# The norms of a half of the heads, computed beside the row sums of a softmax

## The chip, the cores and the metric

The kernel runs on one core of a Trainium2 chip. The metric is the device time of one execution in microseconds (us); the number that counts is the median of several executions of the whole kernel. Everything is in fp32.

## The reference

A transformer layer over `x` of 8 batches, 512 rows and 256 features: attention with 16 heads of 64, in which queries and keys are divided by their norms, and then a gated feed-forward part. Cut to what matters here:

```
def _l2norm(t):
    return t / jnp.maximum(jnp.linalg.norm(t, axis=-1, keepdims=True), 1e-12)
xn = layernorm(x)
q, k, v = heads(xn @ w_q), heads(k of xn @ w_kv), heads(v of xn @ w_kv)
q = _l2norm(q) * jnp.exp(scale)
k = _l2norm(k)
attn = jax.nn.softmax(jnp.einsum('bhid,bhjd->bhij', q, k), axis=-1)
out = heads_joined(jnp.einsum('bhij,bhjd->bhid', attn, v))
x = x + layernorm(out @ w_out + b_out)
x = x + layernorm(ffn(layernorm(x)))
```

So each row of q and of k has one norm for each head, and each row of a softmax has one sum.

## The kernel before, in words

**Tiling and staging.** The attention part comes first, over the 8 batches, and the feed-forward part after it. The 16 heads are 8 head pairs; pairs 0 to 3 are the first half (`hf` 0), pairs 4 to 7 the second (`hf` 1). For a half of a batch there are four projections each of q and k (`qk_step`: product qp or kp in L411, a copy out of PSUM in L422, and its square into a tile called spread). `norms_step` then makes the factors of a half. TensorE multiplies the squares by a mask of halves, with the array in four 32-column tiles (pn_q or pn_k, L456). ScalarE copies the sums out (nd, L480); SyncE folds them by a DMA into a 128x32 tile (nf, L462), VectorE puts a floor under them (L488), GpSimd raises them to the power -0.5 (L312), and for q VectorE multiplies by the scale (L495). SyncE stores the result to DRAM (nq or nk, L502), loads it back spread over the partitions by two DMAs of 512 KB (spread_q or spread_k, L470), and VectorE multiplies the four blocks of qT or kT by it (L512). Scores read only the multiplied blocks.

**Units.** The attention loop runs over units, one for each batch and head pair. In a unit, TensorE gets the first two blocks of scores of the next pair (s, L541), the four blocks of values of this pair (po, L586), in every odd unit the row sums of this pair and the one before it (pd, L609, also in 32-column tiles), the last two blocks of scores of the next pair, and then whatever stands in `plan` for the unit's two slots. ScalarE takes the exponentials of the scores (L555), VectorE adds them up (es, L566). The row sums go through `inverted_two`: the copy d (L623), a fold by DMA (L651), a reciprocal (L671), a store (L657) and two DMAs that spread it (rden, L662), after which VectorE scales oT (L691).

**The plan.** Batch `b` has 16 slots from `base = b * NSLOT`. Projections of the second half stand in slots base - 2 to base + 1. Its norms stand in slot base (q, in unit 0) and base + 2 (k, in unit 1). The scores of pair 4, the first that need the second half, are issued in unit 3. The first half of the next batch is projected and gets its norms in slots base + 6 to base + 9. Slots also hold the output projection of the batch before (pa, L711, L721 to L735, and the store of its rows x1, L759), projections of v (vp, L387), layer norms of the next rows (pt_a, L344), and loads. Over the first batches the slots also hold work on the weights: loads (`looked_at`, L854), tests on VectorE (L861, L866) and `weight_sums`, sums on VectorE (L898) with stores to DRAM (L907). The tile of a sum has two buffers, so the fourth sum of a group waits for an earlier store.

**The order.** Steps are not issued directly. The class `Steps` (L34 to L136) collects them with what they read, write and take. TensorE's order is the order in which they were added; for the other engines and SyncE's queue it plans times from given lengths, and among the steps that are ready it takes the one whose due time, counted back from TensorE's steps, is the earliest. So a step of TensorE that is moved also moves what hangs on it in the orders of the four others. Each engine executes its order strictly. The buffers matter too: the copies d and nd share a pool of two, and pd, pn, pa, vp, qp, kp and pt share a PSUM pool of three.

Of the kernel before, what the change touches and what calls it, by code (L numbers as in the profile page):

```python
# [139 lines left out]
def tile_fast(  # L140
# [50 lines left out]
    NP = H // 2  # L191
# [4 lines left out]
    HP = NP // 2  # L196
# [114 lines left out]
    def power(d, n):  # L311
        nc.gpsimd.tensor_tensor(d, d, neghalf.to_broadcast([P, n]), ALU.pow)  # L312
# [132 lines left out]
    def norms_step(b, hf, which):  # L445

        n = (which, b, hf)
        pn, d, f, r = ("pn", *n), ("nd", *n), ("nf", *n), ("spread", *n)
        to = (which + "T", b, hf)
        r_dram = dram.tile([HH, S], F32, tag=f"n{which}_{b}_{hf}", name=f"n{which}_{b}_{hf}")  # L450
        NF = HH * S // P

        def products():
            tile_of(ps_w, [P, S], "w", pn)
            for j in range(HP):
                nc.tensor.matmul(  # L456
                    T[pn][ts(j, 32), :], lhsT=halves_of, rhs=T[r][:, j, :], start=True, stop=True
                )

        def folded():  # L460
            tile_of(small, [P, NF], "nf", f, bufs=2)
            nc.sync.dma_start(  # L462
                T[f],
                T[d][::16, :].rearrange("i (c n) -> i c n", c=16),
            )

        def spread():
            tile_of(spreadp, [P, HP, S], "spread", r)
            for h in range(2):
                nc.sync.dma_start(  # L470
                    T[r][ts(h, DH)],
                    r_dram.rearrange("(j h) s -> h j s", h=2)[h : h + 1].to_broadcast([DH, HP, S]),
                )

        steps.add(
            "pe", 0.86, products, reads=[(r, j) for j in range(HP)], writes=[(pn, 0)],
            takes=[("w", 3, pn)], tiling=("col", 32),
        )
        steps.add(
            "act", 0.59, lambda: nc.scalar.copy(tile_of(sqp, [P, S], "sq", d), T[pn]),  # L480
            reads=[(pn, 0)], writes=[(d, 0)], takes=[("sq", 2, d)],
        )
        steps.add(
            "sync", 0.1, folded, reads=[(d, 0)], writes=[(f, 0)], takes=[("nf", 2, f)], lag=1.8
        )
        steps.add(
            "dve", 0.12,
            lambda: nc.vector.tensor_scalar_max(T[f], T[f], NORM_FLOOR * NORM_FLOOR),  # L488
            writes=[(f, 0)],
        )  # L490
        steps.add("pool", 6.0, lambda: power(T[f], NF), writes=[(f, 0)])
        if which == "q":
            steps.add(
                "dve", 0.12,
                lambda: nc.vector.tensor_scalar(  # L495
                    T[f], T[f], escale[:, hf : hf + 1], None, ALU.mult
                ),
                reads=[("escale", 0)], writes=[(f, 0)],
            )
        steps.add(  # L500
            "sync", 0.1,
            lambda: nc.sync.dma_start(r_dram.rearrange("i (c n) -> (i c) n", c=16), T[f]),  # L502
            reads=[(f, 0)], writes=[(("rd", *n), 0)], lag=1.5,
        )
        steps.add(
            "sync", 0.2, spread, reads=[(("rd", *n), 0)], writes=[(r, j) for j in range(HP)],
            lag=7.5,
        )
        for j in range(HP):
            steps.add(  # L510
                "dve", 0.69,
                lambda j=j: nc.vector.tensor_tensor(  # L512
                    T[to][:, j, :], T[to][:, j, :], T[r][:, j, :], ALU.mult
                ),
                reads=[(r, j)], writes=[(to, j)],
            )

    def v_step(b, hf, t):
        pm, to = ("vp", b, hf, t), ("v", b, hf)
        projected(pm, b, t, wkv_sb, INNER + hf * HALF)  # L520

        def copied():
            if t == 0:
                tile_of(vp, [P, NT, HALF], "v", to)
            nc.scalar.copy(T[to][:, t, :], T[pm])

        steps.add(
            "act", 0.59, copied, reads=[(pm, 0)], writes=[(to, t)],
            takes=[("v", 2, to)] if t == 0 else (),
        )  # L530
# [109 lines left out]
    def inverted_two(b, p):  # L640

        d = row_sums(b, (p, p + 1), P // 4)
        f, r = ("fold", b, p), ("rden", b, p)
        r_dram = dram.tile([4, S], F32, tag=f"r_{b}_{p}", name=f"r_{b}_{p}")
        T["r", b, p], T["r", b, p + 1] = (r, 0), (r, 1)

        def folded():
            tile_of(small, [P, S // 32], "fold", f, bufs=1)  # L650
            nc.sync.dma_start(  # L651
                T[f],
                T[d][::32, :].rearrange("k (c n) -> k c n", c=32),
            )

        def stored():
            nc.sync.dma_start(r_dram.rearrange("k (c n) -> (k c) n", c=32), T[f])  # L657

        def spread():
            tile_of(esp, [P, 2, S], "rden", r, bufs=1)  # L660
            for h in range(2):
                nc.sync.dma_start(  # L662
                    T[r][ts(h, DH)],
                    r_dram.rearrange("(i h) s -> h i s", h=2)[h : h + 1].to_broadcast([DH, 2, S]),
                )

        steps.add(
            "sync", 0.3, folded, reads=[(d, 0), (d, 1)], writes=[(f, 0)],
            takes=[("fold", 1, f)], lag=1.8,
        )  # L670
        steps.add("dve", 0.2, lambda: nc.vector.reciprocal(T[f], T[f]), writes=[(f, 0)])  # L671
        steps.add("sync", 0.1, stored, reads=[(f, 0)], writes=[(("rd", b, p), 0)], lag=1.5)
        steps.add(
            "sync", 0.3, spread, reads=[(("rd", b, p), 0)],
            writes=[(r, c) for c in range(2)], takes=[("rden", 1, r)], lag=4.0,
        )
# [89 lines left out]
    plan = {}  # L766

    def at(slot, step):
        plan.setdefault(slot, []).append(step)

    def qk_plan(b, hf, slots, norm_slots, between=None):


        for w, some, n in zip("qk", (slots[:HP], slots[HP:]), norm_slots):
            for j, s in enumerate(some):
                at(s, lambda w=w, j=j: qk_step(b, hf, w, j))
            if w == "k" and between:
                at(n, between)
            at(n, lambda w=w: norms_step(b, hf, w))

    def v_plan(b, hf, slots):
        for t, s in enumerate(slots):
# [7 lines left out]
    for b in range(B):  # L790
        base = b * NSLOT
        next_rows(b + 1, base, (0, 2))
        if b:
            qk_plan(b, 1, [base + s for s in (-2, -2, -1, -1, 0, 0, 1, 1)], (base, base + 2))
        next_rows(b + 1, base, (1, 3))
        if b:
            v_plan(b, 1, [base + s for s in (3, 5, 6, 7)])
            for t in range(NT):
                at(base + 2 + t, lambda b=b, t=t: out_proj(b - 1, t))
            n = b - 1 + NX  # L800
            if n < B:
                at(base + 6, lambda n=n: loads(n))
            elif n < B + 2:
                at(base + 6, lambda c=n - B: reloads(c))
        if b + 1 < B:
            qk_plan(
                b + 1, 0, [base + s for s in (6, 6, 7, 7, 8, 8, 9, 9)], (base + 8, base + 9),
                lambda b=b: v_step(b + 1, 0, 0),
            )
            for t in range(1, NT):  # L810
                at(base + 10 + t, lambda b=b, t=t: v_step(b + 1, 0, t))

# [154 lines left out]
    for k, u in enumerate(units):  # L967
        ahead = units[k + 1 : k + 2]
        for jb in range(1, NT):
            summed(*u, jb)  # L970
        for g in range(2):
            for n in ahead:
                for jb in (2 * g, 2 * g + 1):
                    scores(*n, jb)
            if g == 0:
                for jb in range(NT):
                    values(*u, jb)
                if not ahead:
                    for t in range(2):
                        out_proj(B - 1, t, (0, NP - 1), tail=True)  # L980
                b, p = u
                if (b, p // 2) == (B - 1, HP - 1):
                    inverted(b, p)
                elif p % 2:
                    inverted_two(b, p - 1)
        for g in range(2):
            for step in plan.pop(2 * k + g, []):
                step()
        values_out(*u)
        if (b, p // 2) == (B - 1, HP - 1):  # L990
            normalised(b, p)
        elif p % 2:
            normalised(b, p - 1)
            normalised(b, p)
    assert not plan
    for t in range(2, NT):
        out_proj(B - 1, t, (0, NP - 1), tail=True)
    for t in range(NT):
# [1010 lines left out]
```

## Time and profile before

| | |
|---|---|
| median of three runs | 1638.92 us (1638.04 to 1640.67) |
| the profiled execution | 1637.79 us |
| its span | 1636.0 us |
| mean granted TensorE clock | 0.994 |
| busy: TensorE, VectorE, ScalarE, GpSimd | 98%, 62%, 54%, 30% |
| waits of TensorE for keys (L541 for L512) | 10.9 us, 2 times |
| period of a batch, from 305.12 us on | 125.44 us |

Times inside the execution count from the start of the span. A line of the timeline gives the start, the length, engine, line, operation, what is written and read, and the number of instructions taken together; in brackets stands the idle time before it and what ended it. An fp32 product leaves two records, so four products of pn are eight records.

### The profile page before, as it was taken

To read this page: it belongs to the slowest core of one execution; us is meant where nothing else is said; L and a number is where in the kernel's file an instruction comes from. 1 tells how busy PE (TensorE), PEld (TensorE's weight loads), DVE (VectorE), ACT (ScalarE), POOL (GpSimd) and SP (SyncE) were. 2 spreads that over 40 slices of the span, in tenths; PEclk is the share of its full clock that TensorE was granted. 3 is DMA by queue.
4 is the path that set the end of the run, shared out by engine and by line. 5 is a ranking of instruction groups with operands and counts; after the bars stand their busy time and mean duration, and the time that the engine had idled before them with its cause. 6 is when DMAs were issued, how large, how long until landed. Compare 5 with 4: busy or idle time off the path is not lost.

```text
span 1636.0 us, 18863 instructions
## 1 busy us (share of the span) xinstructions
PE 1606.2 (98%) x6808; PEld 916.7 (56%) x6808; DVE 1022.2 (62%) x1708; ACT 878.1 (54%) x1343; POOL 487.6 (30%) x356
## 2 busy tenths in 40 slices
PE   9998989999999999999999999999999999999997
PEld 4332443343353353353353353788888888888886
DVE  3586687454363363364353465869786987879686
ACT  4664535535635535635635534466566646664663
POOL 4211123122122122113112120357155416534451
PEclk9999999999999999999999999999999999999999
DMA  6445455222132122132131231433524532452440
GB/s 176 118 143 154 146 178 147 54 78 67 41 74 65 42 71 67 34 86 57 37 92 47 48 84 35 142 109 136 155 65 130 166 116 78 132 164 65 129 154 28
DMA packets 91042, 159.91 MB, mean 98 GB/s; under 512 B 23868, under 2 KB 39484, under 8 KB 86844
## 3 DMA queue, kind: packets, MB, share of 16 engines
q1 hardware_dynamic: 71324, 95.71, 22.0%
q0 software_dynamic: 18912, 61.87, 12.3%
q8 instruction: 55, 0.90, 0.2%
q10 hardware_dynamic: 704, 1.05, 0.2%
q14 instruction: 47, 0.39, 0.1%
HBM read 140.26 MB, written 17.56 MB: 96 GB/s over the span
## 4 chain that ended last, share of the span: by engine, by line
PE 83%; DVE 2%; issue 1%; DMA 1%; ACT 1%; POOL 0%; SPq 0%; DVEq 0%
PE g L1262 25%; PE s L541 12%; PE po L586 12%; PE p L1188 6%; PE pa L711 6%; PE vp L387 5%; PE kp L411 5%; PE qp L411 5%; PE py L1376 3%; PE pd L609 2%; PE pn_q L456 1%; PE pn_k L456 1%; DMA spread_k<-nk 0%; POOL nf_k L312 0%; PE ptf L1132 0%
## 5 line engine op out<-in xcount | busy, mean ns | idle before, releaser
L555 ACT ACTIVATE e<-s 128x1024 f32<-128x1024 f32 x256 | 248.4, 1021 | 129.6 <-PE s L541 128.7
L541 PE MATMUL s<-qT,kT 64*128 64x512 f32 x1024 | 258.3, 623 | 12.5 <-DVE kT L512 10.9
L586 PE MATMUL po<-e,v 128*64 128x512 f32 x1024 | 235.3, 602 | 0.0
L1262 PE MATMUL g<-h,wb_S 128*128 128x512 f32 x1024 | 234.3, 389 | 0.0
L312 POOL TENSOR_TENSOR nf_q<-nf_q,neghalf 128x32 f32<-128x32 f32 x16 | 87.9, 5494 | 453.6 <-DVE nf_q L488 438.4
L1262 PEld LDWEIGHTS g<-h,wb_S 128*128 128x128 f32 x1024 | 192.0, 188 | 39.8
L566 DVE TENSOR_TENSOR es<-es,e 128x1024 f32<-128x1024 f32 x128 | 156.6, 1224 | 90.0 <-ACT e L555 85.2
L541 PEld LDWEIGHTS s<-qT,kT 64*128 64x128 f32 x1024 | 88.8, 188 | 167.0 <-issue 124.6
L1262 PE MATMUL g<-h,wb_A 128*128 128x512 f32 x768 | 176.4, 389 | 0.0
L1262 PEld LDWEIGHTS g<-h,wb_A 128*128 128x128 f32 x768 | 143.9, 188 | 29.8
L586 PEld LDWEIGHTS po<-e,v 128*64 128x64 f32 x1024 | 68.1, 137 | 160.9 <-issue 158.8
L566 DVE TENSOR_TENSOR es<-e,e 128x1024 f32<-128x1024 f32 x64 | 78.3, 1223 | 116.8 <-PE pd L609 96.3
L1080 DVE TENSOR_TENSOR h<-C,h 128x512 fp32r<-128x512 f32 x112 | 129.6, 1213 | 3.9 <-ACT h L1070 3.8
L1080 DVE TENSOR_TENSOR h<-B,h 128x512 fp32r<-128x512 f32 x112 | 107.9, 1004 | 27.0 <-ACT h L1070 26.7
L312 POOL TENSOR_TENSOR nf_k<-nf_k,neghalf 128x32 f32<-128x32 f32 x16 | 89.3, 5580 | 118.7 <-issue 97.8
L387 PE MATMUL vp<-wkv_sb,aT 128*128 128x512 f32 x256 | 120.6, 602 | 0.0
L711 PE MATMUL pa<-wo_sb,oT 128*128 128x256 f32 x512 | 117.2, 382 | 0.0
L411 PE MATMUL kp<-aT,wkv_sb 128*128 128x512 f32 x256 | 115.8, 601 | 1.4 <-ACT kT L422 1.4
L1318 POOL TENSOR_TENSOR B<-B,B 128x512 f32<-128x512 f32 x64 | 101.9, 1621 | 43.7 <-DVE B L1219 38.8
L411 PE MATMUL qp<-aT,wq_sb 128*128 128x512 f32 (+1 forms) x272 | 114.3, 570 | 0.0
L681 ACT COPY oT<-po 128x512 f32<-128x512 f32 x64 | 37.5, 586 | 141.5 <-PE po L586 141.5
L711 PEld LDWEIGHTS pa<-wo_sb,oT 128*128 128x128 f32 x512 | 95.9, 190 | 31.1 <-issue 17.8
(133 smaller groups left out, 2078.8 us busy)
## 6 DMA issues: line engine op xcount, KB each, us to landing
wb_S<-s POOLq DMA_DIRECT2D x32, 1024.0 KB, 5.2
spread_q<-nq SPq DMA_DIRECT2D x32, 512.0 KB
spread_k<-nk SPq DMA_DIRECT2D x32, 512.0 KB
rden<-r SPq DMA_DIRECT2D x62, 256.0 KB
wb_A<-in_h1T_dram POOLq DMA_DIRECT2D x12, 1024.0 KB, 5.6
wb_A<-in_h2T_dram POOLq DMA_DIRECT2D x12, 1024.0 KB, 5.6
s<-sum SPq DMA_DIRECT2D x32, 256.0 KB
w<-in_h1T_dram SPq DMA_DIRECT2D x8, 512.0 KB
```

Of the source, the lines that this page charges most:

```text
L312: nc.gpsimd.tensor_tensor(d, d, neghalf.to_broadcast([P, n]), ALU.pow)
L387: nc.tensor.matmul(pm, lhsT=T["aT", b][:, c, ts(t, P)], rhs=w[:, c, c0 : c0 + HALF], start=(c == 0), stop=(c == ND - 1),)
L411: nc.tensor.matmul(T[pm][:, cols], lhsT=w[:, c, c0 : c0 + P], rhs=T["aT", b][:, c, cols], start=(c == 0), stop=(c == ND - 1),)
L541: nc.tensor.matmul(T[s][:, h, :], lhsT=T[kT][hp, j, ts(jb, P)], rhs=T[qT][hp, j, :], start=True, stop=True,)
L555: lambda: nc.scalar.activation(tile_of(ep, [P, 2, S], "e", e), T[s], AF.Exp),
L566: nc.vector.tensor_tensor(T[t], T["e", b, p, 0] if jb == 1 else T[t], T["e", b, p, jb], ALU.add)
L586: nc.tensor.matmul(T[po][h * DH : (h + 1) * DH, :], lhsT=T[v][:, jb, c0 : c0 + DH], rhs=T[e][:, h, :], start=(jb == 0), stop=(jb == NT - 1),)
L711: nc.tensor.matmul(banks(), lhsT=T["oT", b, p][:, ts(t, P)], rhs=wo_sb[:, p, :], start=(p == 0), stop=(p == NP - 1),)
L1080: lambda: nc.vector.tensor_tensor(T[h][:, 1, c, :], T[raw][:, c, :], T[h][:, 0, c, :], ALU.subtract),
L1188: nc.tensor.matmul(T[ps[k]], lhsT=(w1r, w2r)[k][c][:, ts(o, P)], rhs=row_halves(b, i)[0][:, c, :], start=(c == 0 and i == 0), stop=(c == N ...
L1262: nc.tensor.matmul(T[to[o]], lhsT=T[w][:, c, ts(o, P)], rhs=T[h][:, i, c, :], start=(first and c == 0 and i == 0), stop=(c == NQ - 1 and i ...
L1318: lambda: (nc.gpsimd if T_ENGINE == "pool" else nc.vector).tensor_tensor(T[dst][:, c, :], T[x][:, c, :], T[y][:, c, :], ALU.subtract),
```

## The change

For the second half of each batch from batch 1 on, the norms of q and of k no longer stand in slots base and base + 2. Both are added directly behind the row sums of pairs 0 and 1, in unit 1 of the batch, so TensorE executes pd, pn_q, pn_k and then the last two blocks of scores. The three groups use the same 32-column tiling. The norms of q come one unit later than before, those of k before two blocks of scores rather than after them. Each step of `norms_step` moves with them. The norms of first halves stay in their slots, and batch 0 is not touched.

```
+    beside = {}
+
+    def qk_plan(b, hf, slots, norm_units, norm_slots):
-        for w, some, n in zip("qk", (slots[:HP], slots[HP:]), norm_slots):
+        for i, (w, some) in enumerate(zip("qk", (slots[:HP], slots[HP:]))):
             for j, s in enumerate(some):
                 at(s, lambda w=w, j=j: qk_step(b, hf, w, j))
-            if w == "k" and between:
-                at(n, between)
-            at(n, lambda w=w: norms_step(b, hf, w))
+            norms = lambda w=w: norms_step(b, hf, w)
+            if norm_units:
+                beside.setdefault(norm_units[i], []).append(norms)
+                continue
+            if w == "k":
+                at(norm_slots[i], lambda: v_step(b, hf, 0))
+            at(norm_slots[i], norms)
...
         if b:
-            qk_plan(b, 1, [base + s for s in (-2, -2, -1, -1, 0, 0, 1, 1)], (base, base + 2))
+            qk_plan(b, 1, [base + s for s in (-2, -2, -1, -1, 0, 0, 1, 1)], (b * NP + 1, b * NP + 1), ())
...
-            qk_plan(
-                b + 1, 0, [base + s for s in (6, 6, 7, 7, 8, 8, 9, 9)], (base + 8, base + 9),
-                lambda b=b: v_step(b + 1, 0, 0),
-            )
+            qk_plan(b + 1, 0, [base + s for s in (6, 6, 7, 7, 8, 8, 9, 9)], (), (base + 8, base + 9))
...
                 elif p % 2:
                     inverted_two(b, p - 1)
+                for step in beside.pop(k, ()):
+                    step()
...
-    assert not plan
+    assert not plan and not beside
```

## The prediction

> **What bounds the kernel now.** I read the page's busy shares and the chain first, to see which engine sets the end.
>
> ```profile
> PE 1606.2 (98%) x6808; PEld 916.7 (56%) x6808; DVE 1022.2 (62%) x1708; ACT 878.1 (54%) x1343; POOL 487.6 (30%) x356
> PE 83%; DVE 2%; issue 1%; DMA 1%; ACT 1%; POOL 0%; SPq 0%; DVEq 0%
> ```
>
> TensorE works 98% of the span, and nearly all of the chain runs through it. So the change can save only what PE itself loses between instructions, and it can cost only where something PE needs comes late. The waits of PE name the one thing that ever came late:
>
> ```profile
> PE s L541 <- DVE kT L512: 10.9, 2, 6.8
> ```
>
> Two scores waited for the scaled keys kT: stall A (6.82 us, before 147.11) and stall B, in batch 1, with this in the timeline of PE and in the table by stretches (after the stretch: length, then busy us of PE, PEld, DVE, ACT, POOL; granted clock, DMA share, GB/s):
>
> ```profile
> 220.36 3.78 PE L541 MATMUL s<-qT,kT 64*128 64x512 f32 x8 [4.13 <-DVE kT L512]
> 216.00:220.00 4.00, 0.23 (x2) 0.00 (x0) 1.52 (x3) 0.00 (x0) 0.00 (x0) 0.97 1.06 307
> 221.00:223.00 2.00, 2.00 (x6) 0.73 (x4) 1.93 (x6) 0.53 (x1) 0.00 (x0) 0.50 0.44 177
> 226.00:227.00 1.00, 1.00 (x6) 0.21 (x4) 0.97 (x3) 0.00 (x0) 0.34 (x1) 0.72 0.03 10
> ```
>
> Eight records of s take 3.78 here and 1.99 elsewhere, because the clock is at half from about 219.9 to 226.4. The second half's pn_q of batches 1 and 2 start at 172.47 and 305.12, 132.65 apart; later ones are 125.44 apart. So stall B costs 7.2: 4.13 of idling and 3.07 of slow clock. Last, the timeline of PE in a steady batch (5), where the change sits:
>
> ```profile
> 681.45 1.07 PE L456 MATMUL pn_q<-spread_q,halves_of 128*32 128x512 f32 x8
> 682.44 3.70 PE L411 MATMUL kp<-aT,wkv_sb 128*128 128x512 f32 x8
> 690.67 1.99 PE L541 MATMUL s<-qT,kT 64*128 64x512 f32 x8
> ...
> 696.17 1.06 PE L609 MATMUL pd<-es,ones 128*32 128x512 f32 x8
> 699.08 1.07 PE L456 MATMUL pn_k<-spread_k,halves_of 128*32 128x512 f32 x8
> 725.14 1.99 PE L541 MATMUL s<-qT,kT 64*128 64x512 f32 x8
> ```
>
> After the change pn_q and pn_k follow pd at once. The s at 725.14 is the first that reads the new qT and kT: it is the deadline. Today pn_q starts 43.7 before it; then it starts 28 before.
>
> **What it saves on PE.** A group in the 32-column tiling (pn or pd, 8 records) starts its successor 0.99 to 1.00 later, each time after a change of tiling. Where no tiling changes, a record streams in 0.428 (vp at 719.88, 4 records, next start 1.71 later); the eight of pn, four side by side, would take 2 x 0.428 = 0.86. So pn_q and pn_k behind pd save 0.14 each. The kp behind pn_q takes 3.54 to its successor, qp behind vp 3.43 (735.38 to 738.81): 0.11 more. Per batch 0.39; bounds 0.11 (a stream behind pd still pays its own start) and 0.45. Seven batches (1 to 7; batch 0's second half lies elsewhere): -2.7, bounds -0.8 and -3.2.
>
> **What a steady batch then has to reach.** u counts from pd's start. The steps after it, each by its row in batch 5 or the next like it: d's copy ends u 1.74 (697.33 and 0.58), the copy of q's norms 2.57; SP issues fold(d), then q's fold 2.60; its floor on VectorE 2.06 behind, 4.66; GpSimd's power 5.42 long, 4.92 to 10.34, k's power right behind it to 16. The two rden loads, now ahead of nq on SP, go out at u 6.1 and land 5.05 later (738.81 to 743.78 gave 4.97; the mean of seven is 5.26), and on VectorE oT times rden stands ahead of q's escale: escale not at 10.4 but at 11.15 + 0.61; so nq is issued at 12.04, spread_q 1.46 later at 13.5. From here batch 0 has the pattern, one spread behind the other (first SP's issues, then VectorE):
>
> ```profile
> 32.75 1.33 SPq L470 DMA_DIRECT2D spread_q<-nq  x2
> 38.47 0.33 SPq L502 DMA_DIRECT2D nk<-nf_k  x1
> 40.47 1.23 SPq L470 DMA_DIRECT2D spread_k<-nk  x2
> ...
> 48.30 2.50 DVE L512 TENSOR_TENSOR kT<-kT,spread_k 128x512 f32<-128x512 f32 x4 [5.48 <-DMA spread_k<-nk]
> ```
>
> Issue to issue 7.72, so spread_k at u 21.2; 7.83 to kT, u 29.05; 0.84 from the first kT to PE (219.52 to 220.36): u 29.9. The deadline is 725.14 - 696.17 = 28.97, plus two pn groups of 0.86 moved in, less the pn_k of 1.00 moved from behind pd's scores: 29.68. (It drifts little: kp and pt of unit 0 lie before pd.) Late by 0.2, or 0.4 with the mean rden of 5.26; I take 0.4, bounds -0.6 (in time) and +1.2, from the spread of the rden rows (4.82 to 5.96) and as much again for the two spreads. Before, the same wait had 725.14 - 719.31 - 0.84 = 5.0 in hand. Six batches (2 to 7): +2.4, from 0 to +7. The late keys hold up only these scores; the clock stays whole at such gaps.
>
> **Here the skill's rule decides.** Today nk at 709.14 is followed by spread_k at 711.54, 2.4 later, with little else in the queue. By that row alone nk, ready at u 16, would free spread_k at 18.4, the scores at 27: no wait, and the sum of the steady batches would be the saving only. "DMA: Bandwidth & Descriptors", Queues, rings and completion order, says that each DMA engine consumes descriptors in the order of the ring; a small store behind a megabyte of spread then waits for all of it. This trace sides with it: the store of a sum issued right behind spread_q released VectorE only 7.0 later.
>
> ```profile
> 187.51 1.25 SPq L470 DMA_DIRECT2D spread_q<-nq  x2
> 188.86 0.55 SPq L907 DMA_DIRECT2D s<-sum  x1
> ...
> 195.83 0.69 DVE L898 TENSOR_TENSOR sum<-w,sum 128x512 f32<-128x512 f32 x1 [8.63 <-DMA s<-sum]
> ```
>
> So I keep 21.2. While nk queues, SP itself stands at the wait before spread_k, and behind it four x1 stores, the load of the next rows and, in batch 1, the weight stores.
>
> **Batch 1.** There weight sums (L898) share VectorE and SP. In the changed order, VectorE's sum_1_2_4 stands ahead of the first qT, and it needs the buffer of sum_1_2_3, whose store stands on SP behind spread_k, an x1 store, a weight load and another x1 store. With pd at 186.06 and the steps above (nq 198.1): spread_q 199.95, spread_k 207.75, the store 210.2. Stores behind a spread released VectorE 8.3 after the spread's issue (187.51 to 195.83) and 8.5 (124.40 to 132.89): with 0.7 for the extra load, about 217. Then sum 0.61, qT 0.61, two additions 2.27, a small one 0.34, three qT 1.85 and 0.84: PE restarts at 223.6. It runs dry at 215.74 (216.23 less the savings): 7.9 idle instead of 4.13. After it the slow clock: "TensorE: Matmul & The Clock Gate", Part 1, gives one window of about 3.4 at half speed, which is 1.7 lost; the rows show 3.07 behind stall B and about 2.2 behind stall A. I take 2.6: 10.5 against 7.2, +3.3 (by the rule +2.4). Bounds: -6.6 (no stall left) and +6. Stall A lies ahead of the change.
>
> **At nothing or nearly.** Batch 2's first half: nk's fold is now issued ahead of nq, spread_q about 1.4 later, against slack of some 0.3 where rows stand around 281: +0.3. POOL's power for the output rows now waits behind k's (5.5): VectorE's L732, ahead of the first qT, then waits to u 16.6, but qT has no data before 21; the exponentials behind k's norm copy on ScalarE wait about 1 us for fold(d), covered by the scores in flight; pd, pn_q and pn_k hold all three buffers of their PSUM pool, but the next takers come at about u 4.6, 8.2 and 9.9, and the copies free them at 1.74, 2.57 and 5.4. Without that cover each would cost about 1 us per batch.
>
> **Sum.** -2.7 + 2.4 + 3.3 + 0.3 = +3.3. The profiled execution took 1637.79 (span 1636.0), 1.1 under the median 1638.92. On the scale of the median: 1642.2, which is the forecast.
>
> **Rivals.** (1) A gain. The decision lies in one wait, sum_1_2_4: if its store lands before spread_k is issued (x1 stores and sums earlier than I reckon), batch 1 keeps kT in time like the steady ones, and the 7.2 of stall B go. Then -2.7 - 6.6 and steady batches on time: about 1630, faster. For it: later batches have slack near zero, not minus 4. Against it: SP is in order, and spread_k stands ahead of the store. 0.17. (2) A draw. The steady batches just make it (spreads 0.5 faster), B grows by 1 to 3: -2.7 + 2 + 0.3, about 1638.5 to 1641; within 0.2%. For it: the miss of 0.4 is within its own error. 0.33. (3) My forecast and its worse end: from 1642.2 on. If each steady batch misses by 1.2, 6 x 1.2 + 3.3 - 2.7 gives +8, 1647. Late from u 29.7 on, each 0.1 costs 0.6. 0.50. That the change does not bring the groups together can't be: the order on PE is fixed, pd, pn_q, pn_k, s.
>
> **How the numbers follow.** 0.2% is 3.3 us, about what a measurement of this kernel can tell from no change. Faster is under 1635.6: rival 1, 0.17. Same 0.33, slower 0.50. The range leaves out rival 1's lower part and the worst tenth: 1634 to 1649. The slower case's own range is 1642 to 1648.
>
> **What would show it.** pd, pn_q and pn_k one behind another with starts about 0.86 apart, and kp without its 0.11; "PE s L541 <- DVE kT L512" with about eight entries, most under 1 us; in batch 1 a stall of 7 to 9 us around 216 to 224 with VectorE held at L898's line by a store, and the clock at half behind it. I am wrong if steady batches never wait (then -2.7 shows whole), if spread_k is issued within 3 of nk's readiness, or if batch 1's stall is under 4.

## The result

The changed kernel takes 1643.76 us (median of 8 runs, 1642.7 to 1645.85) against 1638.85 for the kernel before (8 runs in the same comparison). The ratio is 1.0031, with a 95% interval of 1.0021 to 1.0040: slower by 4.9 us, where 3.3 was forecast. The span of the profiled execution went from 1636.0 to 1641.9.

The page of the changed kernel, busy shares and chain:

```profile
PE 1603.2 (98%) x6808; PEld 918.9 (56%) x6808; DVE 1021.0 (62%) x1708; ACT 878.2 (53%) x1343; POOL 485.9 (30%) x356
PE 42%; issue 30%; POOL 9%; DMA 6%; DVE 5%; ACT 1%; SPq 0%; POOLq 0%; DVEq 0%
```

TensorE's busy time fell by 3.0 us while the span grew by 5.9. The chain now leaves TensorE and runs through GpSimd's powers and the DMAs in the steady batches (2 to 7, in which the work on the weights is over): work off TensorE sets the time there. The waits of TensorE name it:

```profile
PE s L541 <- DVE kT L512: 20.5, 8, 10.2
```

Eight waits instead of two. One is the old stall A before batch 1 (6.62); one is batch 1's stall, now 10.24; six are new, one in each of batches 2 to 7 (0.45, 0.58, 0.71, 0.88, 0.26 and 0.79; called the steady waits below). The timeline of TensorE in batch 5:

```profile
699.70 1.06 PE L609 MATMUL pd<-es,ones 128*32 128x512 f32 x8
700.58 1.04 PE L456 MATMUL pn_q<-spread_q,halves_of 128*32 128x512 f32 x8
701.44 1.04 PE L456 MATMUL pn_k<-spread_k,halves_of 128*32 128x512 f32 x8
702.41 1.99 PE L541 MATMUL s<-qT,kT 64*128 64x512 f32 x8
...
730.34 1.99 PE L541 MATMUL s<-qT,kT 64*128 64x512 f32 x8 [0.88 <-DVE kT L512]
```

The three groups, and the scores behind them, follow one another at 0.88, 0.86 and 0.97: 2.71 together, where the kernel before paid about 2.99 (0.99 to 1.00 for each). The gain that the change is built on is there. It is smaller than the wait in the last line.

Batch 1 in TensorE's timeline and in the stretches (length, busy us of PE, PEld, DVE, ACT and POOL, granted clock, DMA share, GB/s):

```profile
225.56 3.79 PE L541 MATMUL s<-qT,kT 64*128 64x512 f32 x8 [10.24 <-DVE kT L512]
```

```profile
218.00:220.00 2.00, 0.00 (x0) 0.00 (x0) 1.09 (x2) 0.00 (x0) 0.00 (x0) 0.82 0.02 6
224.00:226.00 2.00, 0.45 (x2) 0.48 (x4) 2.00 (x5) 0.00 (x0) 0.00 (x0) 0.50 0.00 0
228.00:230.00 2.00, 2.00 (x8) 0.43 (x6) 1.87 (x7) 1.32 (x2) 1.44 (x2) 0.62 0.00 0
```

The clock falls to half within the stall, at 219.3 by the mean of its stretch (0.82 over 2 us leaves 0.72 at half), and is whole again at 229.5.

**Where the 5.9 us are.** From pd of unit 3 in batch 5 to pd of unit 1 in batch 6 the time fell from 90.97 to 89.78 (pn_q and its switch have left); from pd of unit 1 to pd of unit 3 in batch 5 it rose from 34.47 to 36.14, 0.88 of it the wait. Without the wait that is -1.19 + 0.79 = -0.40 a batch, -2.8 in seven. The six steady waits are +3.67. Batch 1's stall is 6.11 longer (10.24 against 4.13), and the slow clock behind it costs 1.91 instead of 3.01 (the scores and values after it take 7.41 to the next pd, against 8.51 before and 5.50 at full clock): +5.0. The sum is +5.9. Taken from landmark to landmark there are small shifts besides, 0.45 less up to batch 1 and about 0.5 more behind it, which cancel.

### The profile page after: what moved, and what is told of

It reads as the page before. It is cut to its first block, busy times and chain, and to the rows that moved or that the text cites. A ratio compares the mean times of both kernels' runs of the same rounds, so it can differ in the third digit from the quotient of the medians.

```text
span 1641.9 us, 18867 instructions
## 1 busy us (share of the span) xinstructions
PE 1603.2 (98%) x6808; PEld 918.9 (56%) x6808; DVE 1021.0 (62%) x1708; ACT 878.2 (53%) x1343; POOL 485.9 (30%) x356
## 4 chain that ended last, share of the span: by engine, by line
PE 42%; issue 30%; POOL 9%; DMA 6%; DVE 5%; ACT 1%; SPq 0%; POOLq 0%; DVEq 0%
PE g L1267 25%; PE p L1193 6%; POOL nf_k L312 4%; POOL nf_q L312 4%; PE py L1381 3%; DMA spread_k<-nk 3%; PE po L586 3%; DMA nk<-nf_k 2%; PE s L541 2%; DVE es L566 1%; PE pa L711 1%; PE pd L609 1%; PE vp L387 1%; DMA s<-sum 0%; PE kp L411 0%
## 5 line engine op out<-in xcount | busy, mean ns | idle before, releaser
L1323 POOL TENSOR_TENSOR C<-C,C 128x512 f32<-128x512 f32 x64 | 94.1, 1495 | 27.7 <-DVE h L1085 27.2
```

What stands on the lines that cost most here:

```text
L1323: lambda: (nc.gpsimd if T_ENGINE == "pool" else nc.vector).tensor_tensor(T[dst][:, c, :], T[x][:, c, :], T[y][:, c, :], ALU.subtract),
```

## The experiments

Each kernel was compared with the kernel before on the same chip; times are medians, ratios are against the kernel before with their 95% intervals. A profile shows one execution, which can lie off the median.

**One half of the change at a time.** `k_only` keeps q's norms in unit 0, `q_only` keeps k's norms behind the scores of unit 1:

```
-qk_plan(b, 1, [...], (b * NP + 1, b * NP + 1), ())
+qk_plan(b, 1, [...], (None, b * NP + 1), (base, None))        # k_only
+qk_plan(b, 1, [...], (b * NP + 1, None), (None, base + 2))    # q_only
```

> Only k's norms of the second half stand behind the row sums; q's stay in unit 0 as before. My theory (the tiling saves 0.4 us a batch; q's late chain, with k's spread queued behind q's, costs more): the order is pd, pn_k, s, so one change of tiling less, 0.14 to 0.2 us in each of seven batches, about 1 us; k's factors start 3 us earlier than before, so no steady batch waits for kT; batch 1 keeps a stall of about 4 us as before, since SyncE's fold of k's norms still stands behind a store of a weight sum that comes late. Total 1637 to 1639, the kernel before less 1. Rival (any group put behind the row sums jams ScalarE's two copy buffers and the PSUM pool, whichever it is): steady batches wait for kT by some tenths here too, 1640 to 1643.

> Only q's norms of the second half stand behind the row sums; k's stay behind the last two score blocks of unit 1 as before. My theory: q's factors start 14 us later than before and k's spread stays queued behind q's, so the misses of the changed kernel stay whole: 0.3 to 0.9 us in each of the six steady batches and a stall near 10 us in batch 1, where VectorE's fourth sum still stands ahead of qT; saved on TensorE is about 0.3 a batch instead of 0.4. Total 1643 to 1645.5, as the changed kernel or 1 above it. Rival (the two groups together are what is late, because GpSimd's two powers run back to back): with k's norms 3 us later the misses change by more than 1 us a batch either way, 1638 or 1650.

`k_only`: 1642.84 us, ratio 1.0018 (1.0009 to 1.0027). `q_only`: 1644.66, ratio 1.0028 (1.0017 to 1.0039). The waits of TensorE of `k_only`, with its last stall in the timeline, and then the waits of `q_only`:

```profile
PE s L541 <- DVE kT L512: 17.2, 3, 7.6
```

```profile
286.99 3.79 PE L541 MATMUL s<-qT,kT 64*128 64x512 f32 x8 [5.22 <-DVE kT L512]
```

```profile
PE s L541 <- DVE kT L512: 19.8, 8, 6.9
```

(In both, a guard for `None`, not shown, leaves the norms of that half in their slot.)

In which steady batches wait, both came out as expected. `k_only` has no wait from its batch 2's second half on; `q_only` has six, of 0.37 to 2.31, three of them above the 0.9 expected, and its stall in batch 1, 6.25, is shorter than the 10 expected (the profiled execution took 1646.49, the longest of its seven). It is q's move that makes the steady batches late. Both rivals fell: k's group behind the row sums jams nothing, and with k's norms, and so GpSimd's second power, 3 us later the waits stay.

The total of `k_only` was missed by 4 us. Its profiled execution (1645.17, above the median; the 14 lie between 1639.5 and 1647.2) shows something that neither theory had: a third stall of 5.22, ahead of batch 2's first scores. On its VectorE a weight sum waits for a store (ends at 247.89 + 0.69, against 243.49 + 0.69 in the kernel before); the floor of q's norms stands behind it and a row of tests on the weights, at 259.47 instead of 255.06, while pn_q stands at the same place (249.55 and 249.70). A move of the norms also shuffles the weight work in the fixed orders, and here that cost as much as the move itself. So the weight sums had to be taken out of the question.

**The fourth weight sum in place.** It reads the second sum and therefore takes the third sum's buffer, whose store it waits for. Written over the half of the weight tile that it reads, it needs no buffer:

```
-            s = ("sum", n, k, j)
+            s = ("sum", n, k, j) if j < 4 else w2
...
-                nc.vector.tensor_tensor(tile_of(sump, [P, HALF], "s", s), part(x), part(y), op)
+                o = part(x) if j == 4 else tile_of(sump, [P, HALF], "s", s)
+                nc.vector.tensor_tensor(o, part(x), part(y), op)
...
-            ... nc.sync.dma_start(sums_dram[n, j][:, k, :], T[s])
+            ... nc.sync.dma_start(sums_dram[n, j][:, k, :], T[s][:, :HALF])
-                takes=[("s_", 2, s)],
+                takes=[("s_", 2, s)] if j < 4 else (),
```

> The changed kernel, with the fourth weight sum of a group written over the first half of its second weight tile, so that it no longer takes the buffer of the third sum and waits for its store. My theory: in batch 1 VectorE no longer stands before qT until that store has landed behind k's spread; kT is ready when its spread lands, near 217, and the stall of 10.2 falls to 2 to 3.5 with the clock whole, so about 8 to 9 us are gained there; the stall of 6.6 before batch 1 (at 140 to 147), where the fourth sum stands in the same way behind q's spread, falls to 3 or so, 3 to 6 us gained. Steady batches keep their misses of 0.3 to 0.9. Total 1629 to 1633. Rival (in batch 1 it is the spreads themselves that are late, not VectorE): the stall stays over 7 and the total over 1637.

> The kernel before with the same edit of the fourth weight sum. My theory: its stall of 4.1 in batch 1 comes from the same wait one unit earlier (VectorE held 8.6 us until a sum's store lands behind q's spread, and k's fold on SyncE behind it), so it goes entirely, 7.2 us with the slow clock; the stall before batch 1 shrinks as in the changed kernel. Total 1626 to 1629, under the changed kernel with the same edit by 2 to 5: steady misses of 3.7 and what is left of batch 1's stall, less 3 saved on tilings. Rival (stall B of the kernel before is the spread of k itself, late by its place in the plan): it stays near 4, total 1632 to 1635.

The changed kernel so: 1632.33, ratio 0.9945 (0.9932 to 0.9958). The kernel before so: 1620.97, ratio 0.9892 (0.9878 to 0.9906). The waits of the first, and its stall in batch 1:

```profile
PE s L541 <- DVE kT L512: 10.3, 7, 3.6
```

```profile
209.77 3.67 PE L541 MATMUL s<-qT,kT 64*128 64x512 f32 x8 [3.12 <-DVE kT L512]
```

Batch 1's stall fell from 10.24 to 3.12, as expected, but the clock was not whole behind it: the eight records took 3.67, not 1.99. Stall A went entirely, where half was expected; a stall of 3.58 stands before batch 2's first scores, and five steady waits of 0.50 to 0.89 remain. The kernel before has no wait for kT left at all, and is 18 us faster with this edit, 5 below the expected range. Both its stalls went with VectorE's waits for the store of a sum (23.3 us in seven, none left). The rival, late spreads by themselves, fell for the kernel before, and holds for what remains in the changed one (3.12: spread_k goes out at 200.68 and its kT starts at 208.93, with VectorE idle 4.43 for it).

**Only k, sums in place.**

> Only k's norms behind the row sums, and the fourth weight sum in place. My theory: with the weight sums out of the way, k_only's extra stalls (7.6, 4.4 and 5.2 us before batch 1, in it and before batch 2's first scores) go, as they did for the kernel before with the sums in place (1620.97); one change of tiling less in seven batches leaves 1 us: 1619.5 to 1621. Rival (k's group behind the row sums is late by itself, through the copy that waits for the fold of the row sums): a wait for kT in the steady batches, 1623 or more.

1626.43, ratio 0.9930 (0.9908 to 0.9951), but its six runs lie between 1620.9 and 1632.7. The profiled one (span 1620.4) has one wait for kT, of 1.14, ahead of batch 2's first scores, and none in a steady batch. The wide spread was not expected.

**Only k, from batch 2 on, sums in place,** leaves the orders of the weight phase alone:

```
-qk_plan(b, 1, [...], (b * NP + 1, b * NP + 1), ())
+qk_plan(b, 1, [...], (None, b * NP + 1) if b > 1 else (), (base, base + 2))
```

> The fourth weight sum in place, and only k's norms behind the row sums, from batch 2 on; batch 1 as before. My theory: one tiling change less in six batches and no wait for kT from batch 3 on: 0.13 to 0.15 each, 0.8 to 0.9 us under the kernel before with the sums in place, 1620 to 1621; the spread of k_in_place (1620.9 to 1632.7) came from batch 1 and the weight work there, and goes. Rival (the spread comes from k's early norms in every batch): waits for kT in steady batches, or runs over 1626.

1621.54 (1620.43 to 1622.1), ratio 0.9900 (0.9884 to 0.9915). No wait for kT. The period of a batch is 125.30 (from pn_q of a second half, 288.51, to the next, 413.81), against 125.44 with the sums in place alone: 0.14 for the one switch. The median is 0.5 above the expected range and not told apart from that of the sums in place alone: the saving shows in the period only. The spread has gone in these four executions, which points to batch 1 and the weight work; which transfer there varies from run to run stays open.

**The change from batch 2 on,** once with the weight sums as they were and once in place:

```
-qk_plan(b, 1, [...], (b * NP + 1, b * NP + 1), ())
+qk_plan(b, 1, [...], (b * NP + 1, b * NP + 1) if b > 1 else (), (base, base + 2))
```

> The changed kernel with batch 1's norms put back into their old slots, the weight sums untouched: the change in batches 2 to 7 only. My theory: batch 1's stall falls from 10.2 to about 4 with 3 of slow clock behind it, 5 us less than the changed kernel, less 0.4 of tiling that is lost again; the steady waits stay (3.5 to 4 in six batches). Against the kernel before: 6 x 0.42 saved, 3.7 waited, so 0.5 to 2 us slower, 1639 to 1641. Rival (batch 1 is only the first of the late spreads, with the same cause as the others): 1643 to 1644, no gain over the changed kernel.

> The fourth sum in place, and both norms behind the row sums in batches 2 to 7 only; batch 1 as in the kernel before. This is the change without the weight work. My theory: 6 x 0.42 us of tiling and start saved, six waits for kT of 0.3 to 0.9 (sum 3 to 4.5): net +0.5 to +2 against the kernel before with the sums in place, 1621.5 to 1623; waits for kT in six places and nowhere else. Rival (the changed kernel lost only through batch 1): 1618.5, no waits.

`batch_1_as_before`: 1639.6, ratio 1.0004 (0.9995 to 1.0014), within its expectation; the stall of batch 1 is back to 3.91, and four steady waits remain. So what batch 1 adds is about 4 of the 4.9 us, and the steady batches alone come out about even. `both_from_batch_2`: 1623.7, ratio 0.9905 (0.9891 to 0.9919), 2.7 above the kernel before with the sums in place and 0.7 above its expected range. Its profile, of the slowest of the four executions (1626.4), has five waits for kT, only three of them in steady batches (0.84, 0.57 and 1.10); the other two (0.59 and 0.94) stand in batch 1 and ahead of batch 2. "Nowhere else" was wrong.

**Which link makes the steady batches late.** Two kernels take one link each out of `both_from_batch_2`. In the first GpSimd issues nk on its own queue; in the second GpSimd scales q's factors right behind its power, so that VectorE's multiplication no longer stands behind the wait for rden:

```
+        apart = which == "k" and hf and b
         steps.add(
-            "sync", 0.1,
-            lambda: nc.sync.dma_start(r_dram.rearrange(...), T[f]),
+            "pool" if apart else "sync", 1.0 if apart else 0.1,
+            lambda: (nc.gpsimd if apart else nc.sync).dma_start(r_dram.rearrange(...), T[f]),
...
+        def powered():
+            power(T[f], NF)
+            if which == "q":
+                nc.gpsimd.tensor_tensor(T[f], T[f], escale[:, hf : hf + 1].to_broadcast([P, NF]), ALU.mult)
```

> As both_from_batch_2, with one thing more: the store nk of k's factors (16 KB) is issued by GpSimd on its own queue, right behind the power, instead of by SyncE behind spread_q. My theory (nk waits in SyncE's ring until spread_q's megabyte is through, then SyncE needs its 0.5 to 1 us to issue spread_k): nk lands while spread_q runs, spread_k is issued about 3 us after nk, at 18 to 19.5 after the row sums instead of 21.5, its data follows spread_q's without a gap, and the waits for kT vanish: 1618 to 1619.5. Rival (the 16 engines are simply full: the small store waits as long on another queue): spread_k is issued at 21 or later, the waits stay, 1621.5 to 1623.

> As both_from_batch_2, with one thing more: the multiplication of q's factors by the scale is done by GpSimd right behind the power, instead of by VectorE behind the product of oT with rden. My theory (q's factors lie about 1.5 us between the end of the power and VectorE's multiplication, which stands behind a wait for rden): nq goes out 0.5 to 1 us earlier, everything behind it too, and the six waits for kT shrink from 0.3 to 0.9 to 0 to 0.3: 1618.5 to 1620.5. Rival (rden's half megabyte of data holds nq back in the ring, not VectorE): spread_q is issued at the same time after the row sums, 13.8, and the waits stay, 1621.5 to 1623.

`from_2_nk_by_gpsimd`: 1622.78, ratio 0.9905 (0.9891 to 0.9919), as without it. Batch 5 in its timeline of GpSimd and of SyncE, and nk's row in its list of transfers (the last figure is us from issue to landing):

```profile
694.85 0.60 POOL L503 DMA_DIRECT2D nk<-nf_k  x1 [0.29 <-POOL nf_k L312]
```

```profile
692.84 1.25 SPq L470 DMA_DIRECT2D spread_q<-nq  x2
700.70 1.23 SPq L470 DMA_DIRECT2D spread_k<-nk  x2
```

```profile
nk<-nf_k POOLq DMA_DIRECT2D x1, 16.0 KB, 5.8
```

The 16 KB take 5.8 us on a queue of their own, and spread_k still goes out 7.9 behind spread_q: my theory of the ring fell as the explanation. What both cases share is spread_q's megabyte on the DMA engines. The same kernel shows GpSimd's queue without it: in batch 1, where q's norms keep their old slot, spread_q had left 16 us before nk. Here are nk in GpSimd's timeline and in the list of transfers, and then the stretches in which the DMA engines run dry, in batch 1 and in batch 5 (length, PE busy, clock, DMA share, GB/s):

```profile
192.82 0.74 POOL L503 DMA_DIRECT2D nk<-nf_k  x1 [0.31 <-POOL nf_k L312]
nk<-nf_k POOLq DMA_DIRECT2D x1, 16.0 KB, 2.8
```

```profile
194.50:195.00 0.50, 0.50 (x4) 1.00 0.37 125
699.00:699.50 0.50, 0.50 (x6) 1.00 0.46 78
```

In batch 1 it took 2.8, beside the rest of rden's data; in batches 2 to 7 it took 5.1 to 6.3, on the same queue. In each of the seven it landed about 1 us after the engines had run dry. So it is not the queue that is slow: the small store waits while other data fills the engines, whichever queue it is on.

`from_2_scale_by_gpsimd`: 1627.76, ratio 0.9936 (0.9923 to 0.9948). Batch 5 in its timelines of GpSimd and SyncE (pd starts at 685.50), and the stall that it gained:

```profile
695.86 0.24 POOL L494 TENSOR_TENSOR nf_q<-nf_q,escale 128x32 f32<-128x32 f32 x1
```

```profile
696.12 0.32 SPq L504 DMA_DIRECT2D nq<-nf_q  x1
```

```profile
272.09 3.68 PE L543 MATMUL s<-qT,kT 64*128 64x512 f32 x8 [4.01 <-DVE kT L514]
```

nq goes out at 10.62 behind pd, and of the six steady waits one is left, of 0.31; the period is 124.97. This theory held for the steady batches. The total is worse all the same: 1.74 before batch 1 and 4.01 before batch 2 are new. Here every q factor was scaled on GpSimd, first halves and batch 1 too; this run alone does not show that this is the reason, but the last kernel below bears it out.

**The same link alone, in the changed kernel and in the best version.** The scale moves to GpSimd only for second halves from batch 2 on:

```
+        apart = which == "q" and hf and b > 1
...
+            if apart:
+                nc.gpsimd.tensor_tensor(T[f], T[f], escale[:, hf : hf + 1].to_broadcast([P, NF]), ALU.mult)
```

> The changed kernel with one thing more: from batch 2 on, the second half's q factors are scaled by GpSimd right behind the power, not by VectorE behind the wait for rden. Elsewhere nothing is moved, unlike from_2_scale_by_gpsimd, where every q factor was scaled so and the first scores of batch 2 came late. My theory: nq goes out at 10.6 after the row sums instead of 12.3, and the six steady waits of 0.3 to 0.9 vanish; batch 1's stall of 10 stays. Changed kernel less 3.7: 1639 to 1641. Rival (other batches' waits only move to the next late thing): 1642 or more, with waits for qT or for e.

> All that was learnt: the fourth weight sum in place, both norms behind the row sums from batch 2 on, and there the scale by GpSimd right behind the power. My theory: the savings on tilings stay alone in the steady batches, a period near 124.97 instead of 125.44, as from_2_scale_by_gpsimd's profile had it, and nothing is lost around the weights: the kernel before with the sums in place (1620.97) less 6 x 0.45, 1617.5 to 1619.5. Rival (what from_2_scale_by_gpsimd lost in batch 2's first scores comes with the scale's place in the steady batches): 1622 or more.

`changed_scale_by_gpsimd`: 1641.9, ratio 1.0021 (1.0014 to 1.0028). Its waits, and batch 1's stall:

```profile
PE s L553 <- DVE kT L524: 17.6, 5, 9.6
```

```profile
227.11 3.78 PE L553 MATMUL s<-qT,kT 64*128 64x512 f32 x8 [9.57 <-DVE kT L524]
```

Two steady waits remain (0.41 and 0.36) of six: 0.77 against 3.67. The median is 1.9 under the changed kernel's, not 3.7, and so 0.9 above the expected range; a new wait of 0.53 ahead of batch 2 is part of that, and so is stall A, 6.68 long, in the profiled execution, behind which the clock was at half for longer than in the changed kernel (the granted clock of the 20 us from 140 is 0.74 against 0.83).

`best_from_2`, with the sums in place and both norms behind the row sums from batch 2 on: 1619.5 (1618.11 to 1620.46), ratio 0.9885 (0.9868 to 0.9901), the fastest kernel of the study. Its page's busy shares, batch 5 in the timelines of SyncE and TensorE (pd at 677.18), and pn_q of batches 2 and 3:

```profile
PE 1599.8 (99%) x6808; PEld 917.7 (57%) x6808; DVE 1021.1 (63%) x1702; ACT 878.2 (54%) x1343; POOL 486.5 (30%) x362
```

```profile
687.73 0.32 SPq L514 DMA_DIRECT2D nq<-nf_q  x1
689.20 1.24 SPq L470 DMA_DIRECT2D spread_q<-nq  x2
693.10 0.33 SPq L514 DMA_DIRECT2D nk<-nf_k  x1
696.91 1.23 SPq L470 DMA_DIRECT2D spread_k<-nk  x2
```

```profile
706.87 1.99 PE L553 MATMUL s<-qT,kT 64*128 64x512 f32 x8
```

```profile
303.14 1.04 PE L456 MATMUL pn_q<-spread_q,halves_of 128*32 128x512 f32 x8
428.12 1.04 PE L456 MATMUL pn_q<-spread_q,halves_of 128*32 128x512 f32 x8
```

TensorE is busy 99% of the span, nq goes out at 10.55 and spread_k at 19.73 behind pd, the scores find their keys without a wait, and the period is 124.98 (303.14 to 428.12): the 0.46 a batch that the change can give. The new waits of `from_2_scale_by_gpsimd` are gone too, with the scale moved from batch 2 on only. Nearly all of the 19 us against the kernel before comes from the sums in place; against that edit alone the intervals of the ratios overlap, and the change's own share is shown by the period, not by the medians. The two profiles say why: the attention part's last pd starts 2.66 earlier than with the sums in place alone, but the span is only 1.3 shorter. The last pd, the end of two short gaps behind it and a stretch (columns as for the changed kernel) in this kernel, then the last pd with the sums in place alone:

```profile
1002.42 1.08 PE L621 MATMUL pd<-es,ones 128*64 128x512 f32 x4
1023.93 0.50 PE L1204 MATMUL p<-fT,wr 128*128 128x512 f32 x1 [0.99 <-DVE B L1235]
1025.69 0.50 PE L1204 MATMUL p<-fT,wr 128*128 128x512 f32 x1 [0.56 <-ACT sg L1225]
1026.00:1030.00 4.00, 4.00 (x12) 3.12 (x11) 3.56 (x6) 3.18 (x7) 0.00 (x0) 0.57 1.08 345
```

```profile
1005.08 1.08 PE L609 MATMUL pd<-es,ones 128*64 128x512 f32 x4
```

In this execution the clock fell to half for 3.4 us in the feed-forward part, which the change does not touch (0.57 over the 4 us from 1026). It followed the two gaps, of 0.99 and 0.56. The kernel with the sums in place alone has the same two gaps and kept its whole clock there.

## Why the prediction was right, point by point

Every term had the right sign. The saving was sized well, the two costs were too small, and of the links named in the steady chain one, the order within SyncE's ring, does not decide, since another queue was no faster. That the kernel got slower did not hang on the close call of the steady batches, since batch 1 alone outweighs the saving (+5.0 against -2.8); that the loss came out above the 3.3 us which the prediction takes for no change did, since without the steady waits some 2 us would have been left. Within batch 1 two errors partly cancelled: the idling was 2.3 longer than forecast, the slow clock behind it cost 0.7 less.

**The saving** was sized at 0.39 a batch and measured at 0.40, and at 0.46 where nothing is late: the row of the streaming rate (0.428 a record) priced it well. That it could not pay in the changed kernel was the deciding judgement, and it held.

**The steady chain.** Counted from pd in batch 5, forecast and measured: escale on VectorE 11.76 and 12.08, nq 12.04 and 12.34, spread_q 13.5 and 13.80, nk 16 and 15.61, spread_k 21.2 and 21.51, kT 29.05 and 29.80; the deadline of the scores, which start 0.84 behind kT, 29.68 and 29.76. The lines of SyncE and VectorE:

```profile
705.90 1.78 SPq L662 DMA_DIRECT2D rden<-r  x2
712.04 0.32 SPq L502 DMA_DIRECT2D nq<-nf_q  x1
713.50 1.24 SPq L470 DMA_DIRECT2D spread_q<-nq  x2
715.31 0.33 SPq L502 DMA_DIRECT2D nk<-nf_k  x1
721.21 1.23 SPq L470 DMA_DIRECT2D spread_k<-nk  x2
```

```profile
711.17 0.69 DVE L691 TENSOR_TENSOR oT<-oT,rden 128x512 f32<-128x512 f32 x1 [1.79 <-DMA rden<-r]
711.78 0.23 DVE L495 TENSOR_SCALAR nf_q<-nf_q,escale 128x32 f32<-128x32 f32 x1
729.50 2.50 DVE L512 TENSOR_TENSOR kT<-kT,spread_k 128x512 f32<-128x512 f32 x4 [2.40 <-DMA spread_k<-nk]
```

The whole chain came 0.3 late by the wait for rden, and spread_k took 8.29 to the first kT in batch 5, not 7.83. Six waits of 0.61 on average stand where 0.4 was taken: +3.67 for +2.4. The experiments confirm the link that was named, escale behind rden, and weaken the other: nk does wait for spread_q, but a queue of its own didn't free it, so the order within one ring, on which the prediction leaned, is not needed to explain the wait.

**Batch 1** was the term that was sized worst: +3.3 forecast, +5.0 measured. The stall came out at 10.24 for 7.9, the slow clock behind it at 1.91 for 2.6. The mechanism was as described (the row of s<-sum takes two stores together; the first, at 211.63, is the one that the sum waits for):

```profile
218.91 0.69 DVE L901 TENSOR_TENSOR sum<-w,sum 128x512 f32<-128x512 f32 x1 [12.52 <-DMA s<-sum]
```

```profile
208.65 1.24 SPq L470 DMA_DIRECT2D spread_k<-nk  x2
...
211.63 8.32 SPq L910 DMA_DIRECT2D s<-sum  x2
```

The store landed at 218.9, not 217. spread_q went out at 199.67 and spread_k 8.98 behind it, where 7.72 had been taken from a batch without weight traffic. A sum's store of 256 KB had gone out 0.4 ahead of spread_q; at the 219 and 253 GB/s of the stretches from 200 and from 204 us that is an estimated 1.0 to 1.2 us of data. In `sums_in_place_after`, with two such stores beside it, the pair took 9.77 (190.91 to 200.68).

**The slow clock** was weighed between 1.7 (an estimate from the window in the Trainium skill, "TensorE: Matmul & The Clock Gate", Part 1) and the 2.2 to 3.07 of two stalls; 2.6 was taken, and 1.91 measured. Here that estimate was nearer. The half clock ends 4.0 after the restart here and 6.2 after it in the kernel before (0.72 in the last stretch shown there puts its end at 226.56), so one stall's price is not that of the next.

**The small ones.** The first half of batch 2 cost 0.07 instead of 0.3. No new wait of TensorE for PSUM, for ScalarE's copies or for what hangs on GpSimd's row powers appeared. Rival 1, a gain by sum_1_2_4 coming in time, did not occur by itself; `sums_in_place_after` made it so, and 7.1 of the 10.2 us of that stall went, not all: spread_k itself is then what is late.

## What to carry to other kernels

Before work is regrouped to save a switch, count forward from its new place to the first reader: a chain of small transfers with hops between engines can be as long as the slack, and then a saving of 0.4 buys a wait of 0.6. Look in such a chain for an instruction that stands behind a wait for something else in an in-order engine; moving that one instruction to the engine that has the data made the same regrouping pay its 0.46 a batch. And look at background work in the same queues: the sums that waited for a store cost 18 us, more than every part of this change, and moves of other work shifted where they hurt.

## What the runs showed of the hardware

A 16 KB store took 5.1 to 6.3 us on GpSimd's queue while a megabyte of spread was in flight from SyncE's, and 2.8 on the same queue beside less data; with its queue nearly empty SyncE's own nk was followed by its reader 2.4 later. The slow clock came in steps: by the means of the stretches it lasted from 219.28 to 229.52 in the changed kernel (10.24), from 219.76 to 226.56 in the kernel before (6.80), and there in stall A from 144.64 to 151.46 (6.82). These are three and two times 3.41, which is the window that the Trainium skill gives ("TensorE: Matmul & The Clock Gate", Part 1: free-running, 3413 ns). How much of it falls behind the restart is then a matter of phase: 1.91 or 3.01 lost, with the longer stall losing less. Nor does it take a long stall: after the two gaps of 0.99 and 0.56 in the feed-forward part, `best_from_2` (1026.25 to 1029.65), `q_only` and `batch_1_as_before` show one such step of 3.4 at half clock, while the other profiles have the same gaps there and no step. And the same pair of spreads took 7.57 to 8.15 from issue to issue in the steady batches of the changed kernel, and 8.98 in batch 1 beside the store of a sum.
